# Gates kept in PSUM, a list schedule with new costs that picks engines, and a residual folded into a weight, in a four-layer graph network

## The chip, the cores and the metric

The kernel runs on one core of a Trainium2 chip. The metric is device time in microseconds (us). Its engines are TensorE (PE in the views; PEld is its weight load), VectorE (DVE), ScalarE (ACT), GpSimd (POOL) and SyncE (SP), which here only issues DMA. "Span" is the time from the first to the last instruction in the profiled execution; "median" is over the timed runs.

## The reference, cut to what matters

The input is 64 graphs of 256 nodes by 128 features, fp32, with one adjacency matrix. Four layers follow each other, each inside a residual and a layer norm:

```python
x = _layernorm(x + _L0_gnn_ref(x, adj, adj, ...))   # gated cell, five steps
x = _layernorm(x + _L1_gnn_ref(x, adj, ...))        # graph convolution, softmax adjacency
x = _layernorm(x + _L2_gnn_ref(x, adj, ...))        # attention, then an MLP
x = _layernorm(x + _L3_gnn_ref(x, adj, adj, ...))   # Chebyshev terms up to order 3
# one step of layer 0:
u3 = h @ u3_w.T + u3_b
z  = sigmoid(av @ w3_w.T + w3_b + u3)
r  = sigmoid(av @ w4_w.T + w4_b + u3)
hv = tanh(av @ w5_w.T + w5_b + (r * h @ u5_w.T + u5_b))
h  = (1.0 - z) * h + z * hv
```

In this case's data, the layer-2 parameters gat_g are all one and gat_b all zero.

## The kernel before

The kernel works on 32 pairs of graphs. It does not write its instructions in the order of the program: it adds each operation to a graph with an engine, a cost in ns, and the buffers it reads, writes and takes. Then a list scheduler in the kernel's own Python plays the program through with those costs and fixes the order of every engine's queue:

```python
LATENCY = {PE: 230, ACT: 80, DVE: 80, POOL: 120, SP: 1800}
...
    def order(self):
        ...
                for op in waiting[e]:
                    at = max(op.ready, clock[e])          # when it could start, in the model
                    ...
                    key = (at, op.rank)                   # earliest first, then the longest tail
            ...
            clock[op.eng] = at + op.cost
            end = at + op.cost + op.lat
```

On the chip each engine takes its queue strictly in that order, and semaphores hold an instruction back until its inputs are there. So a wrong cost gives no wrong result, only a queue whose head may wait while ready work stands behind it. A step of layer 0, cut:

```python
            tv, hv = bank(), flat("hv")                    # a PSUM bank; an SBUF tile
            add(PE, 865, ... matmul(tv.ap, w5s.ap, mT.ap ...), [mT, w5s], [tv], [tv, hv])
            add(PE, 865, ... matmul(tv.ap, u5h.ap, tr.ap ...), [tr, u5h], [tv])
            add(ACT, 690, ... activation(hv.ap, tv.ap, AF.Tanh, bias=bh.ap), [tv, bh], [hv])
            add(DVE, 735, ... tensor_sub(hv.ap, hv.ap, hT.ap), [hT], [hv])
            add(DVE, 735, ... scalar_tensor_tensor(hv.ap, tz.ap, 1.0, hv.ap, ...), [tz], [hv])
            add(DVE, 735, ... scalar_tensor_tensor(hT.ap, hv.ap, 0.5, hT.ap, ...), [hv], [hT])
            h = turn(add, hT, wide("htok"))                # VectorE transpose, then four DMAs
```

The new state of a step goes through `turn`: VectorE transposes in blocks, and SyncE issues four DMAs that put the blocks in place.

## Time and profile before

| | before |
|---|---|
| median | 1550.74 us of three runs (1551.2 of four beside the result, 1552.8 to 1553.2 beside the experiments) |
| PE / DVE / ACT / POOL busy | 98% / 71% / 63% / 31% |
| matmul records at the pace of their width | 1510.3 us |
| first matmul starts at | 5.9 us |
| gaps between records: to 150, 150 to 1250, 1250 to 1450, after 1450 us | 4.5, 1.3, 4.5, 18.3 us |
| from the last matmul's slot to the end | 6.3 us |

The last four rows add up to the span. A gap is what lies between the starts of two successive matmul records beyond the pace of the first one's width: 0.8333 ns a column plus 3.2 ns, which is within about 2 ns of the measured 429, 215 and 112 ns. All gaps below are worked out so from the start times in the traces.

### The profile page before, as it was taken

The page shows a single profiled execution, that of the slowest core. Times are in us where ns is not written, and L with a number is a line of the kernel's source. Part 1 is how long each engine was busy: PE and PEld are TensorE (multiplying, and loading weights), DVE is VectorE, ACT ScalarE, POOL GpSimd, SP SyncE. Part 2 cuts the span into 40 slices and gives each one's busy share as a digit, 9 for nine tenths or more (in the row PEclk, how much of TensorE's full clock was granted, in tenths as well). Part 3 has the DMA queues.
Part 4 walks back from the last instruction along what each step waited for, and adds up shares of the span by engine and source line. Part 5 has one row for each costly group of instructions (what it writes and reads, how often), then busy time and mean ns, then how long its engine had stood idle before and what let it go on. Part 6 is the DMA issues. An engine that isn't in the chain of part 4 may idle for free.

```text
span 1551.2 us, 21563 instructions
## 1 busy us (share of the span) xinstructions
PE 1522.9 (98%) x6364; PEld 1060.9 (68%) x6364; DVE 1106.7 (71%) x2579; ACT 972.0 (63%) x2198; POOL 487.1 (31%) x532
## 2 busy tenths in 40 slices
PE   8999999999999999999999999999999999999797
PEld 5556666667776676676676766676766776766686
DVE  4688776777666776666877666867667776877775
ACT  3344666666666676665766666666666666766663
POOL 0001232343323343223433223433223333423464
PEclk9999999999999999999999999999999999999999
DMA  7224445454355545445553556454445445545210
GB/s 246 43 35 64 72 75 79 80 93 80 65 89 101 90 72 92 74 87 93 91 88 58 91 88 102 75 93 76 78 89 89 77 77 86 95 74 83 42 22 28
DMA packets 725368, 125.33 MB, mean 81 GB/s; under 512 B 707844, under 2 KB 708612, under 8 KB 725124
## 3 DMA queue, kind: packets, MB, share of 16 engines
q1 hardware_dynamic: 724964, 123.42, 46.4%
q8 instruction: 52, 0.85, 0.2%
q14 instruction: 64, 0.52, 0.1%
q10 hardware_dynamic: 288, 0.53, 0.1%
HBM read 27.86 MB, written 8.45 MB: 23 GB/s over the span
## 4 chain that ended last, share of the span: by engine, by line
PE 94%; DVE 2%; POOL 1%; DMA 1%; SPq 1%; issue 0%; ACT 0%; POOLq 0%; DVEq 0%
PE ps L535 18%; PE ps L632 10%; PE ps L567 9%; PE ps L549 9%; PE ps L557 9%; PE ps L565 9%; PE ps L552 9%; PE ps L645 7%; PE ps L868 7%; PE ps L819 3%; PE ps L880 3%; PE ps L743 2%; SPq L515 1%; DMA sd<-line 1%; DVE u L780 0%; POOL rs L697 0%
## 5 line engine op out<-in xcount | busy, mean ns | idle before, releaser
L697 POOL TENSOR_TENSOR rs<-ss,neg_half 128x4 f32<-128x4 f32 (+1 forms) x140 | 155.5, 1111 | 518.6 <-DVE ss L690 509.9
L571 DVE TENSOR_TENSOR hv<-hv,hT 128x512 f32<-128x512 f32 x160 | 111.3, 696 | 184.9 <-ACT hv L569 184.0
L535 PE MATMUL ps<-aTs,htok 128*128 128x256 f32 x1024 | 242.3, 380 | 0.7 <-DMA htok<-S 0.5
L535 PEld LDWEIGHTS ps<-aTs,htok 128*128 128x128 f32 x1024 | 194.2, 190 | 62.5 <-issue 31.8
L538 ACT COPY mix<-ps 128x512 f32<-128x512 f32 x160 | 92.4, 583 | 156.6 <-PE ps L535 155.0
L567 PE MATMUL ps<-tr,u5h 128*128 128x512 f32 x320 | 163.4, 593 | 3.1 <-DVE tr L562 3.0
L552 PE MATMUL ps<-mix,w4s 128*128 128x512 f32 x320 | 163.1, 593 | 0.4 <-ACT mix L538 0.4
L557 PE MATMUL ps<-mix,dw 128*128 128x512 f32 x320 | 163.3, 593 | 0.0
L555 ACT ACTIVATE tr<-ps,br 128x512 f32<-128x512 f32 x160 | 109.0, 681 | 81.4 <-PE ps L552 76.3
L565 PE MATMUL ps<-mix,w5s 128*128 128x512 f32 x320 | 159.9, 593 | 0.0
L549 PE MATMUL ps<-hT,W 128*128 128x512 f32 x320 | 159.4, 593 | 0.0
L562 DVE SCALAR_TENSOR_TENSOR tr<-tr,hT 128x512 f32<-128x512 f32 x160 | 111.6, 698 | 44.2 <-ACT tr L555 43.5
L572 DVE SCALAR_TENSOR_TENSOR hv<-tz,hv 128x512 f32<-128x512 f32 x160 | 115.7, 723 | 35.2 <-ACT tz L560 33.7
L569 ACT ACTIVATE hv<-ps,bh 128x512 f32<-128x512 f32 x160 | 109.5, 684 | 48.9 <-PE ps L567 48.8
L560 ACT ACTIVATE tz<-ps,bz 128x512 f32<-128x512 f32 x160 | 109.9, 688 | 30.5 <-PE ps L557 30.1
L574 DVE SCALAR_TENSOR_TENSOR hT<-hv,hT 128x512 f32<-128x512 f32 x160 | 116.4, 728 | 2.2
L635 ACT COPY mix<-ps 128x512 f32<-128x512 f32 (+1 forms) x105 | 57.5, 549 | 89.0 <-PE ps L632 89.0
L509 DVE STREAM_TRANSPOSE S<-hT 128x512 f32<-128x512 f32 x160 | 109.9, 696 | 0.6
L552 PEld LDWEIGHTS ps<-mix,w4s 128*128 128x128 f32 x320 | 60.3, 190 | 54.3 <-issue 45.1
L688 DVE TENSOR_REDUCE ss<-sq 128x4 f32<-128x512 f32 (+1 forms) x140 | 85.9, 622 | 11.7 <-ACT sq L685 11.2
L645 PEld LDWEIGHTS ps<-W,mix 128*128 128x128 f32 x512 | 74.6, 192 | 28.2 <-issue 25.3
L663 POOL TENSOR_SCALAR rs<-mv 128x4 f32<-128x4 f32 (+1 forms) x70 | 31.1, 444 | 189.4 <-DVE mv L659 187.0
(213 smaller groups left out, 2964.3 us busy)
## 6 DMA issues: line engine op xcount, KB each, us to landing
htok<-S SPq DMA_DIRECT2D x640, 64.0 KB
xT<-S SPq DMA_DIRECT2D x232, 64.0 KB
wT<-S SPq DMA_DIRECT2D x116, 128.0 KB
xs<-xs_in SPq DMA_DIRECT2D x32, 256.0 KB
hT<-xT_in SPq DMA_DIRECT2D x32, 256.0 KB
dT<-S SPq DMA_DIRECT2D x116, 64.0 KB
sd<-line SPq DMA_DIRECT2D x29, 256.0 KB
zT<-S SPq DMA_DIRECT2D x116, 64.0 KB
```

What stands on the lines that cost most here:

```text
L535: nc.tensor.matmul(t.ap[:, b * N:(b + 1) * N], src.ap[:, 2 * b + j, :], m.ap[:, j, :], start=(j == 0), stop=(j == 1))
L549: add(PE, 865, lambda tg=tg: nc.tensor.matmul(tg.ap, mat("u3"), hT.ap, start=True, stop=False, skip_group_check=True), [hT, W0], [tg], [tg ...
L552: add(PE, 865, lambda tg=tg, mT=mT: nc.tensor.matmul(tg.ap, w4s.ap, mT.ap, start=False, stop=False, skip_group_check=True), [mT, w4s], [tg])
L557: add(PE, 865, lambda tg=tg, mT=mT: nc.tensor.matmul(tg.ap, dw.ap, mT.ap, start=False, stop=True, skip_group_check=True), [mT, dw], [tg])
L562: add(DVE, 735, lambda tr=tr: nc.vector.scalar_tensor_tensor(tr.ap, tr.ap, 1.0, hT.ap, op0=ALU.add, op1=ALU.mult), [hT], [tr])
L565: add(PE, 865, lambda tv=tv, mT=mT: nc.tensor.matmul(tv.ap, w5s.ap, mT.ap, start=True, stop=False), [mT, w5s], [tv], [tv, hv])
L567: add(PE, 865, lambda tv=tv, tr=tr: nc.tensor.matmul(tv.ap, u5h.ap, tr.ap, start=False, stop=True), [tr, u5h], [tv])
L572: add(DVE, 735, lambda hv=hv, tz=tz: nc.vector.scalar_tensor_tensor(hv.ap, tz.ap, 1.0, hv.ap, op0=ALU.add, op1=ALU.mult), [tz], [hv])
L574: add(DVE, 735, lambda hv=hv: nc.vector.scalar_tensor_tensor(hT.ap, hv.ap, 0.5, hT.ap, op0=ALU.mult, op1=ALU.add), [hv], [hT])
L632: nc.tensor.matmul(t.ap[:, b * N:(b + 1) * N], src.ap[:, 2 * b + j, :], m.ap[:, j, :], start=(j == 0), stop=(j == 1))
L645: nc.tensor.matmul(t.ap[:, c * D:(c + 1) * D], s(c), w, start=(k == 0), stop=(k == len(terms) - 1))
L697: nc.gpsimd.tensor_tensor(rs.ap, ss.ap, neg_half.ap[:, :C], op=ALU.pow)
```

## The change

Its intent was to give the scheduler better numbers and more freedom. Costs now follow the distance between starts of back-to-back instructions; a shared port of VectorE and GpSimd is modelled; some operations may run on either of two or three engines; the candidate gate stays in PSUM; layer 3's residual becomes an identity inside a weight; and the last pairs are handled differently.

```diff
-N_TAIL = 3
+N_TAIL = 2
-LATENCY = {PE: 230, ACT: 80, DVE: 80, POOL: 120, SP: 1800}
+EXTRA = [0, 0, 600, 0, 0]
+LATENCY = {PE: 205, ACT: 140, DVE: 130, POOL: 85, SP: 1800}
 def place(p):
-    return 20000 * min(p, 27) + 6000 * max(p - 27, 0)
+    return 20000 * min(p, 23) + 6000 * max(p - 23, 0)
     # in order(): the port, and operations that may go to several engines
+                    if entry[4]:
+                        at = max(at, shared - entry[4][0])
...
+            if port:
+                shared = at + sum(port)
     # layer 3: the residual within the weight
-        nc.vector.tensor_copy(vx.ap[:, 0, :], mat("v0"))
+        nc.vector.tensor_add(vx.ap[:, 0, :], mat("v0"), unswap.ap)
     # costs (some of many)
-            return 150 + 1.055 * n      # VectorE
-            return 250 + 0.745 * n + 93 * aps   # ScalarE
+        return 75 + 1.042 * n
+        return 100 + 0.8 * n + 93 * aps
-        add(DVE, 510 * C + 360, f, [sd, h2, mask], [u, mx, nm])
+        add(DVE, 415 * C + 280, f, [sd, h2, mask], [u, mx, nm], port=not by_pe)
-        add(ACT, 691 * C, f, [nm], [u, rd])
+        add(ACT, 491 * C, f, [nm], [u, rd])
     # layer 0: the candidate gate in PSUM
-            add(ACT, 690, ... activation(hv.ap, tv.ap, AF.Tanh, bias=bh.ap), [tv, bh], [hv])
-            add(DVE, 735, ... tensor_sub(hv.ap, hv.ap, hT.ap), [hT], [hv])
+            add(ACT, 545, ... activation(tv.ap, tv.ap, AF.Tanh, bias=bh.ap), [bh], [tv])
+            add(DVE, 609, ... tensor_sub(tv.ap, tv.ap, hT.ap), [hT], [tv])
     # engine choice, an example
-        add(POOL, 200 + 2.3 * C * D, lambda: nc.gpsimd.tensor_add(y.ap, x_t.ap, row("l1_bias", C)), ...)
+        two(add, C * D, lambda e: e.tensor_add(y.ap, x_t.ap, row("l1_bias", C)), ...)   # VectorE or GpSimd
```

## The prediction

> **What bounds the kernel now.** I read the page's busy times first, then who TensorE (PE) waited for, then the stretches, then the chain of the last 50 us.
>
> ```profile
> PE 1522.9 (98%) x6364; PEld 1060.9 (68%) x6364; DVE 1106.7 (71%) x2579; ACT 972.0 (63%) x2198; POOL 487.1 (31%) x532
> ```
>
> PE at 98% need not mean full speed, because matmuls are pipelined and their ends are modelled. So I took the start times of all 6364 matmul records. A record of 512 columns is followed by the next after 0.429 us (median), one of 256 columns after 0.215, one of 128 or 130 after 0.112. An fp32 product is two such records, so 512 columns cost 0.86 us, which the chain shows too:
>
> ```profile
> 1322.72 0.86 PE ps L567 x2
> 1323.58 0.86 PE ps L565 x2
> 1324.44 3.45 PE ps L868 x16
> ```
>
> Taking every record at the pace of its width, the sum is 1510.3 us (1600 of 512 columns, 2816 of 256, 1931 of 128 or 130). The rest of the 1551.2 us: the first matmul starts at 5.9 us, behind the load of the adjacency; 28.7 us are gaps between records beyond their pace; and from the last matmul's slot to the end of the span it takes 6.3 us (evacuation, norm, store). 1510.3 + 5.9 + 28.7 + 6.3 = 1551.2, which closes.
>
> In 50 us bins the gaps are: 4.5 us in the first 150 us (few pairs started); 1.3 us in all from 150 to 1250; 4.5 us from 1250 to 1400; 18.3 us after 1450. The stretches show the same:
>
> ```profile
> 400.00:600.00 200.00, 200.00 (x836) 139.86 (x835) 137.65 (x314) 128.59 (x289) 62.80 (x60) 1.00 0.49 84
> 1250.00:1300.00 50.00, 49.46 (x235) 37.39 (x234) 32.60 (x72) 32.22 (x75) 19.27 (x19) 1.00 0.55 90
> 1300.00:1350.00 50.00, 48.05 (x213) 34.19 (x213) 43.65 (x114) 38.33 (x95) 20.89 (x25) 1.00 0.48 80
> 1450.00:1480.00 30.00, 21.89 (x135) 19.10 (x135) 25.64 (x89) 19.29 (x57) 16.93 (x26) 0.89 0.20 35
> 1510.00:1520.00 10.00, 6.63 (x29) 5.29 (x29) 7.86 (x27) 3.90 (x11) 9.42 (x18) 0.84 0.01 2
> ```
>
> Columns after the length: busy us of PE, weight load, VectorE, ScalarE, GpSimd (records), granted clock, DMA share, GB/s. From 400 to 600 us PE is never idle, while VectorE is at 69% and ScalarE at 64%. It is idle at the end, where VectorE is the busy one (85% of 1450 to 1480), and from 1510 to 1520 GpSimd (94%). PE's own waits name the same places:
>
> ```profile
> PE ps L632 <- DVE x_t L669: 6.6, 2, 5.4
> PE ps L535 <- DMA aTs<-adjs_in: 5.9, 1, 5.9
> PE ps L567 <- DVE tr L562: 3.0, 2, 1.9
> PE ps L632 <- ACT hg L828: 2.9, 1, 2.9
> ```
>
> The largest is one wait of 5.4 us for a normalized tile that stood in VectorE's queue; the fourth is for a relu whose input came from GpSimd. So the kernel is bound by PE's arithmetic, plus a tail in which the last pairs' chains are too few and VectorE and GpSimd too busy.
>
> **What the Trainium skill says.** "Perfetto Trace Analysis", section Identifying the Most-Contended Engine, calls matmul busy time a poor measure and LDWEIGHTS busy a good one. Here they are 98% and 68%, and the start-to-start times side with the 98%: the 68% is no headroom. "TensorE: Matmul & The Clock Gate", section "Wait — 56ns, not 53.3ns?", gives a warm start-to-start of N / 2.4 GHz plus about 2.5 ns; an fp32 record here steps 429 ns at 512 columns, which fits if a record is two passes (2 x 213.3 + 2.5 = 429.2). The granted clock is 1.00, so only fewer matmuls or fewer gaps can help. "SBUF — State Buffer", section Who interferes with whom, says that a VectorE instruction with two SBUF inputs contends with a GpSimd instruction that reads SBUF, and that with at most one SBUF input (outside the two-port modes) it does not. The trace agrees in direction:
>
> ```profile
> L826 POOL TENSOR_TENSOR hg<-hg,rbc 128x512 f32<-128x512 f32 x29 | 46.9, 1618 | 2.3
> L727 POOL TENSOR_TENSOR y<-x_t,rbc 128x512 f32<-128x512 f32 x29 | 37.6, 1297 | 124.9 <-ACT x_t L678 101.0 <-DMA xT<-S 17.8 <-DMA htok<-S 6.1
> L574 DVE SCALAR_TENSOR_TENSOR hT<-hv,hT 128x512 f32<-128x512 f32 x160 | 116.4, 728 | 2.2
> L730 DVE TENSOR_TENSOR y<-ps,y 128x512 f32<-128x512 f32 x29 | 19.3, 667 | 9.6 <-PE ps L645 9.6
> ```
>
> The same GpSimd shape takes 1297 to 1618 ns, and VectorE's 128x512 takes 728 ns with both inputs in SBUF against 667 with one in PSUM. "ScalarE: Activation LUTs", section "Step-by-step: what each stage is for", says that ScalarE writes to PSUM with less latency than to SBUF. The kernel before has no such write, so no run shows it yet.
>
> **The change, part by part.**
>
> *PE work.* No matmul of a normal pair goes or comes. The residual of layer 3 becomes an identity added to a weight, in set-up; the product has the same shape. Only N_TAIL from 3 to 2 counts: a tail pair transposes on PE, per half-pair 4 x 2 tiles, 2 score columns and 4 attention tiles, so 14 one-record transposes, 28 a pair, at 0.112 us = 3.1 us; its four smaller products of layer 3 add under 0.1 us. PE's sum becomes 1510.3 - 3.2 = 1507.1.
>
> *Gates in PSUM.* Per step the tanh of the candidate is written in place and three VectorE operations take it from there. At 0.03 to 0.06 us saved on each (728 or 696 against 667), 160 steps x 3 x 0.045 = 22 us of VectorE's 1107, all beside PE: worth nothing where PE is gap-free. The price is the PSUM bank. Averaged over 160 steps, the tanh ends at 695.3 us and the last VectorE operation on it at 700.5, so a bank is held 5.2 us longer per step: 160 x 5.2 / 1551 = 0.54 of 8 banks on average. The step's banks hold now 3.4 (mix), 12.9 (gates) and 6.4 us (candidate), 22.7 us in all, 2.3 banks on average; layers 1 to 3 use some more. I expect no new wait from it.
>
> *Residual and evacuations.* The 58 additions of 415 ns (24 us, VectorE) become copies that ScalarE or VectorE may make; copies of mixes (51 + 92 us, ScalarE) may go to VectorE. Again beside PE, except in the tail.
>
> *Engine choice.* Adds and scalings can go to GpSimd, VectorE or ScalarE, whichever ends first in the model, with 600 ns against VectorE. That takes from VectorE in the tail, where PE waited for it, and from GpSimd the scale-and-shift pairs that it does alone now (1541 + 1618 ns a pair in a row).
>
> *Costs in the model.* The largest part, I think. The order of every queue is static and comes from these costs. The old ones overstate: 735 ns for a gate operation, where the timeline shows VectorE stepping by about 600 when it is not held; 691 ns for an exponential of 256 columns, now 491, where the timeline steps by 0.49 us. A schedule made with too slow VectorE and ScalarE is harmless where PE has a backlog and wrong where the chains are short, which is the tail. The last nine pairs instead of the last five are brought close in priority, so that more chains are open at the end.
>
> The sum: 1507.1 + 5.9 + 6.3 = 1519.3 us with no gap at all. Then the gaps: start 4.5 to 4 (cold clock and first loads stay); middle 1.3 to 1.5; 1250 to 1400 from 4.5 to 1.7; the tail from 18.3 to 6.5. That is 13.7 us, a choice of mine: the first two are set by loads and few open pairs, the last two by queues that the change aims at, so I halve them and a bit more. 1519.3 + 13.7 = 1533.0 us, 1.1% less.
>
> **Rivals.** (1) *PSUM becomes the bound.* If bursts fill the 8 banks, PE waits in the gap-free middle; 0.1 us a step would give back 16 us: 1549. Against it: 0.54 bank on average, and a scheduler that counts banks. (2) *Port contention.* More GpSimd operations beside VectorE's two-input ones lengthen both; GpSimd is the slower engine, about 1.3 us a tile against 0.7. If the tail's chains go through it, the tail keeps its 18 us and only the transposes are saved: 1551 - 3 - some 4 = 1544. For it: GpSimd was already 94% busy from 1510 to 1520. Against: the model now has the port. (3) *The tail is closed almost wholly*: gaps of 6 us, 1525. For it: at 85% VectorE has room as soon as some 5 us of its work goes elsewhere. (4) *Fewer tail pairs cost latency*: the third last pair now turns its tiles by DMA, and a score row's way through DMA takes over 4 us; if that pair ends last, 5 us come back: 1538.
>
> **Range and chances.** The floor of 1519.3 is all but 2% below 1550.7 (1519.7), so over 2% faster would need no gap or less arithmetic: 0.03. Slower by over 2% (above 1581.7) would need 62 us of new gaps, more than twice those of now: 0.02. Range 1523 to 1546.
>
> **What would show it right or wrong.** PE's records should sum to about 1507 us; the stretch 400 to 600 should still be 100% busy, or rival 1 holds; PE's idle time after 1450 should fall from 18 to below 10 us, or rival 2; VectorE should lose some 40 us and GpSimd gain. I am wrong if the middle gets gaps, or if the tail is as long as before.

## The result

The changed kernel takes 1592.8 us (median of four, 1589.8 to 1592.9) against 1551.2, so it is slower. The ratio is 1.0263, with a 95% interval of 1.0245 to 1.028. Ratios here are the mean time of one kernel's runs over that of the other's runs of the same rounds, so they are not quite the ratio of the medians quoted. The prediction, 1533 within 1523 to 1546 and at 95% "within 2%", was wrong.

The page's busy line and the start of its chain, after the change:

```profile
PE 1532.0 (96%) x6328; PEld 1047.1 (66%) x6328; DVE 1193.2 (75%) x2649; ACT 878.4 (55%) x1890; POOL 462.7 (29%) x538
...
PE 59%; DVE 21%; SPq 6%; DMA 5%; POOL 4%; issue 3%; ACT 2%; DVEq 0%; POOLq 0%; ACTq 0%
```

And the start of the chain before the change:

```profile
PE 94%; DVE 2%; POOL 1%; DMA 1%; SPq 1%; issue 0%; ACT 0%; POOLq 0%; DVEq 0%
```

Before, the chain that ended last was PE and hardly anything else. Now 36% of it runs through VectorE, the DMA queue, DMA and GpSimd. Busy time alone hides this: 96% still looks like a bound PE. VectorE gained 86 us of busy time, where I had expected it to lose 40; ScalarE lost 94, and GpSimd, which was to gain, lost 24.

The stretches after the change (length, then busy us and records of PE, PEld, DVE, ACT, POOL; clock; DMA share; GB/s):

```profile
400.00:600.00 200.00, 190.42 (x780) 129.58 (x780) 152.91 (x324) 107.34 (x226) 61.98 (x66) 1.00 0.48 80
1000.00:1200.00 200.00, 200.00 (x768) 131.61 (x767) 136.99 (x278) 109.79 (x224) 41.32 (x45) 1.00 0.45 74
...
1450.00:1500.00 50.00, 49.82 (x233) 37.64 (x232) 37.47 (x92) 29.70 (x64) 22.97 (x29) 1.00 0.48 73
1500.00:1550.00 50.00, 49.17 (x287) 43.26 (x286) 38.34 (x127) 35.11 (x99) 26.60 (x41) 1.00 0.29 55
```

From 400 to 600 us PE ran 780 records where it had run 836, at the same clock. The tail, on the other hand, is as tight as hoped. One stretch of the middle, 1000 to 1200, has no gap at all; there GpSimd did a third less than from 400 to 600. In terms of the sum:

| us | before | predicted | after |
|---|---|---|---|
| records at pace | 1510.3 | 1507.1 | 1507.2 |
| first matmul | 5.9 | 5.9 | 6.1 |
| gaps to 150 | 4.5 | 4 | 8.4 |
| gaps 150 to 1250 | 1.3 | 1.5 | 47.6 |
| gaps 1250 to 1450 (predicted: to 1400) | 4.5 | 1.7 | 8.1 |
| gaps after 1450 | 18.3 | 6.5 | 8.0 |
| end | 6.3 | 6.3 | 5.8 |

Who PE waited for, after the change (us, times, longest):

```profile
PE ps L613 <- DVE tr L608: 29.2, 25, 1.6
PE ps L920 <- ACT mix L561: 6.3, 11, 1.3
PE ps L581 <- DMA aTs<-adjs_in: 6.1, 1, 6.1
```

L613 is the product that needs r * h, which VectorE makes in L608. Its wait comes back about once in 49 us, at the pace of one pair. At 500.5, 548.8, 599 and so on the same product is up to 1.8 us late, each time behind the layer-3 products.

### Where one of these waits comes from

The kernel's scheduling routine gives each operation a planned start. I ran that routine and laid the plan beside the trace: the operations of each engine come in the same order in both, so every one can be matched. The before kernel's plan ends at 1549.2 us; PE stays within about 6 us of it all the way. The changed kernel's plan ends at 1530.2 us; PE is 10 us late at a planned 174 us, 26 at 481, 49 at 962, and 58 at 1520, so most of the loss falls in the first two thirds.

The wait at 500.5 us goes back to PE itself, 39 us before. Along that loop (times in us, "late" is actual minus planned):

```
                                            planned   actual    late
PE    L932 layer-3 product, ends             439.2    461.9     22.7
DVE   L608 gate of another pair, ends        446.3    469.2     22.9
DVE   L832 masked maximum, ends              449.4    473.1     23.8
DVE   L894 relu plus residual, ends          451.8    476.3     24.5
SP    L539 four DMA issues (wT), end         460.3    485.3     25.0
SP    L539 four DMA issues (xT), end         463.0    488.5     25.5
SP    L539 four DMA issues (htok), end       465.7    491.3     25.5
DVE   L764 addition on that htok, starts     467.5    493.6     26.1
DVE   L608 the gate waited for, ends         474.5    500.4     25.9
PE    L613                        starts     474.9    500.5     25.6
```

So one round adds 2.9 us, read along this chain. About 0.9 are VectorE's masked maximum, 0.7 another VectorE operation, and some 1.6 DMA issue and landing; a few tenths come back where latencies were overstated. As the loop closes through PE, nothing makes it up, and the next round adds its own.

The VectorE part, instruction by instruction (timeline of VectorE, then of GpSimd; start, us, engine, line):

```profile
469.11 1.49 DVE L832 CUSTOM_DVE_ANT_0 u<-sd,maskb 128x256 f32<-128x256 f32 x1
...
470.53 1.48 DVE L832 CUSTOM_DVE_ANT_0 u<-sd,maskb 128x256 f32<-128x256 f32 x1
...
471.94 0.41 DVE L832 CUSTOM_DVE_ANT_0 u<-sd,maskb 128x256 f32<-128x256 f32 x1
```

```profile
468.67 1.65 POOL L876 TENSOR_TENSOR hg<-hg,rbc 128x512 f32<-128x512 f32 x1 [0.80 <-DVE hg L749]
470.39 1.33 POOL L877 TENSOR_TENSOR hg<-hg,rbc 128x512 f32<-128x512 f32 x1
```

The same instruction takes 0.41 us alone and 1.49 while GpSimd is on a two-input operation; the first two end about when GpSimd's do. The model has a port, but as a lock held for a whole operation, and it lets the next operation on it start only when the one before is planned to end. Here GpSimd's first operation was planned at 1.24 us and took 1.65, so L832's first instruction still met it. L832 is one operation to the scheduler and ten instructions on the chip; GpSimd's second operation, planned behind all ten, got in between them. Over the whole run the groups were, before and after:

```profile
L780 DVE CUSTOM_DVE_ANT_0 u<-sd,maskb 128x256 f32<-128x256 f32 x116 | 47.3, 463 | 23.3 <-DMA sd<-line 23.2
L842 DVE SCALAR_TENSOR_TENSOR hb<-hb,y 128x512 f32<-128x512 f32 x29 | 20.4, 704 | 1.0
```

```profile
L832 DVE CUSTOM_DVE_ANT_0 u<-sd,maskb 128x256 f32<-128x256 f32 x120 | 81.0, 728 | 0.5 <-DMA sd<-line 0.2
L894 DVE SCALAR_TENSOR_TENSOR hb<-hb,y 128x512 f32<-128x512 f32 x30 | 34.7, 1155 | 0.1
```

As a group, the masked maximum of a full pair was planned at 2.40 us before and took 2.07 on average; after, it was planned at 1.94 and took 3.20.

The DMA part (SyncE's queue):

```profile
481.60 3.68 SPq L539 DMA_DIRECT2D wT<-S  x4
485.39 3.10 SPq L539 DMA_DIRECT2D xT<-S  x4
488.60 2.65 SPq L539 DMA_DIRECT2D htok<-S  x4
```

Four issues are planned at 2.73 us; these took 3.68, 3.10 and 2.65 (mean over the run 2.84, and 2.78 before). The landing is planned at 1.80; here the consumer started 2.4 us after the last issue ended (median of the consumers that sat waiting 1.9). The means are hardly different before, where PE was not held up: there one wait of 0.5 us on such a transfer is all that PE shows.

### The profile page after: what moved, and what is told of

The parts are those of the page before. It is cut to its first block, busy times and chain, and to the rows that moved or that the text cites. A ratio compares the mean times of both kernels' runs of the same rounds, so it can differ in the third digit from the quotient of the medians.

```text
span 1591.2 us, 21200 instructions
## 1 busy us (share of the span) xinstructions
PE 1532.0 (96%) x6328; PEld 1047.1 (66%) x6328; DVE 1193.2 (75%) x2649; ACT 878.4 (55%) x1890; POOL 462.7 (29%) x538
## 4 chain that ended last, share of the span: by engine, by line
PE 59%; DVE 21%; SPq 6%; DMA 5%; POOL 4%; issue 3%; ACT 2%; DVEq 0%; POOLq 0%; ACTq 0%
PE ps L581 13%; PE ps L613 6%; SPq L539 6%; PE ps L598 5%; PE ps L595 5%; PE ps L603 5%; PE ps L672 5%; PE ps L611 4%; PE ps L920 4%; DMA htok<-S 4%; PE ps L685 4%; DVE S L533 3%; PE ps L932 3%; PE ps L871 2%; DVE ps L618 2%
## 5 line engine op out<-in xcount | busy, mean ns | idle before, releaser
L561 ACT COPY mix<-ps 128x512 f32<-128x512 f32 (+1 forms) x253 | 145.1, 574 | 220.4 <-PE ps L581 141.5
L613 PE MATMUL ps<-tr,u5h 128*128 128x512 f32 x320 | 168.0, 607 | 29.2 <-DVE tr L608 29.2
L744 POOL TENSOR_SCALAR ss<-ss 128x4 f32<-128x4 f32 (+1 forms) x102 | 23.5, 231 | 482.5 <-DVE ss L736 482.4
L745 POOL TENSOR_TENSOR rs<-ss,neg_half 128x4 f32<-128x4 f32 (+1 forms) x136 | 135.6, 998 | 75.2 <-DVE ss L738 66.6
L608 DVE SCALAR_TENSOR_TENSOR tr<-tr,hT 128x512 f32<-128x512 f32 x160 | 119.9, 749 | 46.9 <-ACT tr L601 42.6
L616 ACT ACTIVATE ps<-ps,bh 128x512 f32<-128x512 f32 x160 | 104.1, 651 | 87.5 <-PE ps L613 87.4
L617 DVE TENSOR_TENSOR ps<-ps,hT 128x512 f32<-128x512 f32 x160 | 109.8, 686 | 43.3 <-ACT ps L616 41.3
L618 DVE SCALAR_TENSOR_TENSOR ps<-tz,ps 128x512 f32<-128x512 f32 x160 | 109.5, 686 | 20.8 <-ACT tz L606 19.1
L613 PEld LDWEIGHTS ps<-tr,u5h 128*128 128x128 f32 x320 | 56.7, 189 | 100.2 <-DVE tr L608 57.8
L620 DVE SCALAR_TENSOR_TENSOR hT<-ps,hT 128x512 f32<-128x512 f32 x160 | 108.6, 680 | 2.7
```

Of the source, the lines that this page charges most:

```text
L561: add(ACT, act(n) - 45, lambda: nc.scalar.copy(o(), i()), *args).also = [(DVE, dve(n), lambda: nc.vector.tensor_copy(o(), i()), None)]
L608: add(DVE, 609, lambda tr=tr: nc.vector.scalar_tensor_tensor(tr.ap, tr.ap, 1.0, hT.ap, op0=ALU.add, op1=ALU.mult), [hT], [tr], port=True)
L613: add(PE, 865, lambda tv=tv, tr=tr: nc.tensor.matmul(tv.ap, u5h.ap, tr.ap, start=False, stop=True), [tr, u5h], [tv])
L617: add(DVE, 609, lambda tv=tv: nc.vector.tensor_sub(tv.ap, tv.ap, hT.ap), [hT], [tv])
L618: add(DVE, 609, lambda tv=tv, tz=tz: nc.vector.scalar_tensor_tensor(tv.ap, tz.ap, 1.0, tv.ap, op0=ALU.add, op1=ALU.mult), [tz], [tv])
L745: nc.gpsimd.tensor_tensor(rs.ap, ss.ap, neg_half.ap[:, :C], op=ALU.pow)
```

## The experiments

The theory (T): the new costs are close to an undisturbed start-to-start time, so the plan has no margin. It fills queues so that any instruction longer than planned, by a collision or by a late DMA, reaches PE. Rivals: the candidate gate holds PSUM banks too long; the new engine mix is at fault, not the costs; DMA alone; or the changed order is just an unlucky draw. Each run had three rounds, with the kernel before timed on the same chip, and each gave a correct result.

### e1: the gate back in SBUF, same order

```diff
-            tv = bank()
+            tv, hv = bank(), flat("hv")
-            add(ACT, 545, ... activation(tv.ap, tv.ap, AF.Tanh, bias=bh.ap), [bh], [tv])
+            add(ACT, 545, ... activation(hv.ap, tv.ap, AF.Tanh, bias=bh.ap), [tv, bh], [hv])
     # and the three VectorE operations on hv, costs unchanged
```

> The changed kernel with the candidate gate back in SBUF: the scheduler's order on every engine is the very same list (I compared the two lists), only the storage of the tanh and of three VectorE operands differs. If the longer hold of PSUM banks is what stalls TensorE (rival 1 of the prediction), the time falls towards 1535. If the cause is the order made with tight costs, it stays at about 1593, or rises by up to 10 us because VectorE's three operations per step then have two SBUF inputs and meet GpSimd on the port.

Measured: 1613.3 us, ratio 1.0388 (1.0371 to 1.0406). The PSUM rival falls: in this order, the gate in PSUM is worth 20 us (1613.3 less 1592.8), twice as much as I had allowed for. Its gaps add up to 92.3 us. Two of the groups that changed, changed kernel and then this one:

```profile
L608 DVE SCALAR_TENSOR_TENSOR tr<-tr,hT 128x512 f32<-128x512 f32 x160 | 119.9, 749 | 46.9 <-ACT tr L601 42.6 <-DMA dT<-S 4.1
L618 DVE SCALAR_TENSOR_TENSOR ps<-tz,ps 128x512 f32<-128x512 f32 x160 | 109.5, 686 | 20.8 <-ACT tz L606 19.1
```

```profile
L608 DVE SCALAR_TENSOR_TENSOR tr<-tr,hT 128x512 f32<-128x512 f32 x160 | 127.4, 796 | 44.3 <-ACT tr L601 44.3
L618 DVE SCALAR_TENSOR_TENSOR hv<-tz,hv 128x512 f32<-128x512 f32 x160 | 113.5, 710 | 22.2 <-ACT tz L606 20.7
```

With both inputs in SBUF again L618 is only 24 ns longer on average, but its longest takes 1756 ns, where none took over 737 with one input in PSUM. L608, which the edit does not touch and which PE waits for, grows more: 19 of its 160 take over 900 ns in both runs, 15 or 16 of them beside one GpSimd operation (L749), and those take about 1195 ns in the changed kernel and 1566 here. That this is what cost the 20 us is read from the traces, not tested.

### e2: a margin of 15% on VectorE, ScalarE and GpSimd

```diff
-            op = g.add(eng, cost, fn, (p, n[0]), reads, writes, takes)
+            op = g.add(eng, cost if eng in (PE, SP) else cost * 1.15, fn, (p, n[0]), reads, writes, takes)
     # and the same factor on the costs of an operation's other engines
```

> The changed kernel, with only the scheduler's costs of VectorE, ScalarE and GpSimd operations times 1.15 (engine choice, port model, gates in PSUM, place and N_TAIL as changed). Theory T (the new costs leave no margin, so whatever takes longer than modelled reaches TensorE once a round): the gaps of 45.6 us from 150 to 1200 us fall below 5 us and the time is 1530 to 1545, below the kernel before. Contention theory (the new mix of GpSimd and VectorE work is the cause): more work goes to GpSimd, so it stays above 1575. PSUM theory: stays at about 1590.

Measured: 1557.5 us, ratio 1.0031 (1.0016 to 1.0046). The direction is T's and the contention theory's 1575 is missed, though GpSimd was given more to do. But I had expected 1530 to 1545: gaps of 16.8 us stayed from 150 to 1250. In the loops behind them, as I traced them back, the largest overrun is now DMA issue (19 us), which had been given no margin. So T needed an addition, that the margin must cover the DMA too; e8 tests it.

### e3: the same order, two GpSimd operations cut to one column

```diff
-        two(add, C * D, lambda e: e.tensor_mul(hg.ap, hg.ap, row("gat_g", C)), [rbc], [hg])
-        two(add, C * D, lambda e: e.tensor_add(hg.ap, hg.ap, row("gat_b", C)), [rbc], [hg])
+        two(add, C * D, lambda e: e.tensor_mul(hg.ap[:, :, :1], hg.ap[:, :, :1], row("gat_g", C)[:, :, :1]), [rbc], [hg])
+        two(add, C * D, lambda e: e.tensor_add(hg.ap[:, :, :1], hg.ap[:, :, :1], row("gat_b", C)[:, :, :1]), [rbc], [hg])
```

> The changed kernel in the same order, but the two GpSimd operations that scale and shift by gat_g and gat_b touch one column in 128 only (gat_g is one and gat_b zero, so the result stays right). That takes away the long two-input GpSimd reads beside VectorE's masked maximum (3.20 us a group of ten instructions against 1.94 modelled). If port contention starts the stall, that group falls to about 2.1 us and the time by some 15 to 25 us, to 1568 to 1578. If DMA alone does, it stays above 1588.

Measured: 1565.2 us, ratio 1.0078 (1.0063 to 1.0093); 28 us off, a little more than expected. The plan is the same list, so nothing but the durations can have done it. The masked maximum is back to 1.9 us a group, as planned:

```profile
L832 DVE CUSTOM_DVE_ANT_0 u<-sd,maskb 128x256 f32<-128x256 f32 x120 | 44.7, 427 | 0.3 <-DMA sd<-line 0.3
```

L894 is back at 726 ns as well. What stays, 22.0 us of gaps from 150 to 1250, is again behind DMA issue, as far as the trace tells. This is no fair kernel, since it leans on the data. It also makes the two operations themselves shorter (about 1440 ns to 360), which could have helped in its own right. A replay speaks against that. It is an estimate: it lets each operation of the plan's order start when its engine, its inputs and its buffers are free, with durations from the traces. With the changed kernel's own durations it ends at 1603 us (the chip: 1591), with e3's durations for GpSimd alone at 1604, and with e3's for VectorE alone at 1573. So, by this estimate, e3 measures the collision.

### e4: tight costs, engines as before

```diff
-        op = add(*a, *args)
-        op.also, op.port = [(*b, (60, pool(n) - 80))], (75, dve(n) - 75)
+        op = add(*(b if on == POOL else a), *args)
+        op.port = (60, pool(n) - 80) if on == POOL else (75, dve(n) - 75)
     # on=POOL for the four operations that were on GpSimd; no operation keeps an alternative
```

> The changed kernel with the tight costs, but no engine choice: every operation on the engine that it had before (additions of layer 3's residual still gone). Theory T: the middle still has gaps, time 1560 to 1600. If the engine choice alone is the fault: 1530 to 1540, the middle gap-free.

Measured: 1580.1 us, ratio 1.0175 (1.0156 to 1.0193). 27 us of loss stay without the engine choice, so the mix alone is not the cause. The 13 us between this run and the changed kernel are not the price of the choice, because the order is another one too: gaps from 150 to 1250 are down to 24.3 us, but those from 1250 to 1450 are up to 22.5.

### e5: the kernel before, with only the costs of the change

```diff
-LATENCY = {PE: 230, ACT: 80, DVE: 80, POOL: 120, SP: 1800}
+LATENCY = {PE: 205, ACT: 140, DVE: 130, POOL: 85, SP: 1800}
-            add(DVE, 735, ...)
+            add(DVE, 609, ...)
     # and so on for every cost that the change touched; nothing else
```

> The kernel before, with nothing changed but the scheduler's costs and latencies, which are those of the change (engines, gates in SBUF, N_TAIL 3, place 27 as before). Its own list schedule then expects 1539.5 us in place of 1549.2. Theory T (tight costs are enough to lose): slower than before, 1565 to 1600, with gaps from 150 to 1250 us of over 15 us where the kernel before has 1.3. If the tight costs are harmless and the new engine mix is at fault: 1540 to 1552.

Measured: 1583.5 us, ratio 1.0194 (1.0172 to 1.0216). Numbers that no instruction ever sees, only the scheduler, cost 30 us. Gaps from 150 to 1250 are 18.5 us where the kernel before has 1.3; they also grow at the start (9.3), from 1250 to 1450 (9.2) and in the tail (22.0). This is the clearest run that tight costs alone lose time. It does not single out one collision. The masked maximum is as short as before (448 ns against 463); here it is r * h (L562) that meets GpSimd: 23 of its 160 take over 900 ns, 22 of them beside the same GpSimd operation (L826). Before, and then e5:

```profile
L562 DVE SCALAR_TENSOR_TENSOR tr<-tr,hT 128x512 f32<-128x512 f32 x160 | 111.6, 698 | 44.2 <-ACT tr L555 43.5
```

```profile
L562 DVE SCALAR_TENSOR_TENSOR tr<-tr,hT 128x512 f32<-128x512 f32 x160 | 132.6, 829 | 92.0 <-ACT tr L555 92.0
```

The same replay as in e3 ends at 1582 us with this run's durations (the chip: 1581.5). As estimates from it: r * h kept to 690 ns wins back 1.5 us, DMA issue as planned 5, and all VectorE operations kept to their planned cost 23. So many overruns on VectorE share the loss, and which of them a tight order exposes differs from order to order.

### e6: the kernel before, with only the gate in PSUM

The edit is e1's the other way round, on the kernel before, with its costs of 690 and 735.

> The kernel before, with only the candidate gate kept in PSUM (costs as before; the scheduler's order comes out identical). Every theory left says that the middle has no gap to win, so 1549 to 1553; less in the tail at most. If PSUM gates cost banks it would be above 1556.

Measured: 1551.8 us, ratio 0.9988 (0.9973 to 1.0003), no difference. The order is the same list as before. Where PE has no gap, shorter VectorE work is worth nothing; in e1's order it was worth 20 us.

### e7: the DMA charged in full, costs still tight

```diff
-LATENCY = {PE: 205, ACT: 140, DVE: 130, POOL: 85, SP: 1800}
+LATENCY = {PE: 205, ACT: 140, DVE: 130, POOL: 85, SP: 2450}
-        add(SP, 2730, f, [S], [dst], [dst])
+        add(SP, 2900, f, [S], [dst], [dst])
```

> The changed kernel, with only the DMA of a turn modelled as the trace has it: 2.90 us for its four issues in place of 2.73, and 2.45 us to landing in place of 1.80. If the DMA's underestimate is the main cause, 1540 to 1560. If VectorE's collisions with GpSimd are the main one, as the run with the cut GpSimd work said (28 us of 42), it gains under 15 us: 1578 to 1595.

Measured: 1560.1 us, ratio 1.0045 (1.003 to 1.006). My expectation was wrong: it gained 33 us, not under 15. I had also called the numbers "as the trace has it", while they are near its slower cases (means 2.84 and 1.9). They are a margin on the DMA. But this run does not isolate the DMA, because the order is a new one. The masked maximum takes 462 ns here instead of 728, so most of its collisions went as well. Gaps from 150 to 1250 are 13.6 us.

### e8: both margins

The edits of e2 and e7 together.

> The changed kernel with both: costs of VectorE, ScalarE and GpSimd times 1.15 and the true DMA of a turn. In the run with the margin alone, the chains behind the 21 us of remaining gaps from 150 to 1450 us held 19 us of DMA issue time over the model. If that is right, they mostly close: 1535 to 1548, faster than the kernel before.

Measured: 1539.0 us, ratio 0.9907 (0.989 to 0.9923), faster than the kernel before by 0.9%, and 54 us faster than the changed kernel with only costs edited. The middle is full again:

```profile
400.00:600.00 200.00, 200.00 (x838) 139.84 (x837) 140.53 (x310) 118.78 (x249) 66.60 (x71) 1.00 0.50 85
```

VectorE has 70% and GpSimd 33% to do here, more on GpSimd than in the changed kernel (31%). So it is not the amount of GpSimd work that decides, but when it meets VectorE and how much room there is.

### e9: tight costs in another order

```diff
-N_TAIL = 2
+N_TAIL = 3
-    return 20000 * min(p, 23) + 6000 * max(p - 23, 0)
+    return 20000 * min(p, 27) + 6000 * max(p - 27, 0)
```

> The changed kernel with N_TAIL 3 and place 27 as before, all else as changed: again tight costs, but another order (its own schedule expects 1538.3 us). Theory T: the middle stalls as well, 20 to 60 us of gaps from 150 to 1200 us, 1575 to 1605 in all. If the changed order was only an unlucky draw, this one is near 1545.

Measured: 1607.5 us, ratio 1.0351 (1.0336 to 1.0367), just above the expected range. Gaps from 150 to 1250 are 54.3 us. So the changed order was not a single unlucky draw: another tight one loses as much in the middle, and e4 and e5 are two more that lose.

### e10: the kernel before, with only the tail's numbers

The edit of e9 the other way round, on the kernel before.

> The kernel before with only N_TAIL 2 and place 23 of the change, loose costs kept (its own schedule expects 1545.2 us against 1549.2). The transposes' 3.2 us go and the middle stays gap-free: 1544 to 1549. If the DMA latency of the third last pair ate it, 1550 or more.

Measured: 1549.3 us, ratio 0.9976 (0.9959 to 0.9993). The transposes' 3.2 us are won, and no more. The gaps after 1450 fall from 18.3 to 3.2 us, but those from 1250 to 1450 rise from 4.5 to 18.5, with waits for the turned state on top (here with the loose costs; 8.5 of the 9.2 us fall from 1250 to 1450):

```profile
PE ps L535 <- DMA htok<-S: 9.2, 6, 4.0
```

So with old costs, the new placing only moved the tail's wait to an earlier place, some 150 us before.

### e11 and e12: a larger margin, and one aimed at the collision

e11 is e8 with 1.20 in place of 1.15. e12 is e8 with one more edit:

```diff
-        add(DVE, 415 * C + 280, f, [sd, h2, mask], [u, mx, nm], port=not by_pe)
+        add(DVE, 415 * C + 1280, f, [sd, h2, mask], [u, mx, nm], port=not by_pe)
```

> As the run with margin 1.15 and the true DMA (1539.0), margin 1.20. Its own schedule expects 1537.6 in place of 1532.7. If the margin is already enough at 1.15, more of it only dulls the tail: 1538 to 1548.

> As the run with margin 1.15 and the true DMA, and the masked maximum charged 1 us more, about what it lost to GpSimd in the changed kernel (3.20 against 1.94 us). Of the 20 us of gaps left, 3.5 are from 150 to 1450 chains and some 6 lie before 150: at most 3 us are to be won: 1535 to 1543.

Measured: e11 1548.8 us, ratio 0.9973 (0.9958 to 0.9988); e12 1536.5 us, ratio 0.9895 (0.988 to 0.9909), the lowest median of all; e11 is just above its expected range. More margin everywhere lost 10 us, and not in the tail as I had written, but in the middle (9.6 us of gaps from 150 to 1250). There r * h collides again: from 330 to 946 us PE waits 0.4 to 1.8 us for it once a pair, 14 times, each time after an L608 of about 1.38 us beside a GpSimd operation. e8, and then e11:

```profile
L608 DVE SCALAR_TENSOR_TENSOR tr<-tr,hT 128x512 f32<-128x512 f32 x160 | 117.4, 734 | 63.3 <-ACT tr L601 58.7
```

```profile
L608 DVE SCALAR_TENSOR_TENSOR tr<-tr,hT 128x512 f32<-128x512 f32 x160 | 124.7, 780 | 49.7 <-ACT tr L601 49.4
```

So a margin does not see to it that the collisions fall where they do no harm, and the amount of it has to be tried. e12's median is 2.5 us below e8's, but that is not shown as a gain: the intervals of the two ratios overlap, the runs were on different chips, and the order is a new one. e12's last stretches:

```profile
1450.00:1500.00 50.00, 50.00 (x301) 45.53 (x300) 36.42 (x119) 33.51 (x95) 31.39 (x46) 1.00 0.26 54
1500.00:1534.00 34.00, 25.07 (x143) 21.57 (x141) 16.87 (x54) 13.43 (x36) 15.64 (x30) 0.95 0.07 24
```

Its sum is 1507.2 + 5.8 + 15.6 of gaps + 5.8 = 1534.3 us, the profiled span.

### All of them beside their own plan

| run | plan ends | median | plan missed by | gaps 150 to 1250 |
|---|---|---|---|---|
| before | 1549.2 | 1551 to 1553 | 2 to 4 | 1.3 |
| after | 1530.2 | 1592.8 | 63 | 47.6 |
| e1 gate in SBUF | 1530.2 | 1613.3 | 83 | 61.6 |
| e2 margin 1.15 | 1533.0 | 1557.5 | 25 | 16.8 |
| e3 GpSimd cut | 1530.2 | 1565.2 | 35 | 22.0 |
| e4 old engines | 1531.7 | 1580.1 | 48 | 24.3 |
| e5 before, tight | 1539.5 | 1583.5 | 44 | 18.5 |
| e6 before, gate in PSUM | 1549.2 | 1551.8 | 3 | 0.0 |
| e7 DMA charged | 1530.3 | 1560.1 | 30 | 13.6 |
| e8 margin and DMA | 1532.7 | 1539.0 | 6 | 1.6 |
| e9 tight, tail 3 | 1538.3 | 1607.5 | 69 | 54.3 |
| e10 before, tail 2 | 1545.2 | 1549.3 | 4 | 2.6 |
| e11 margin 1.20 and DMA | 1537.6 | 1548.8 | 11 | 9.6 |
| e12 margin, DMA, collision | 1535.8 | 1536.5 | 1 | 1.8 |

"Plan ends" is what each kernel's own scheduling routine returns. The plans with loose costs, or with margin and DMA both, come true within 11 us; those with tight costs miss by 35 to 83, and those with only one of the two margins (e2, e7) by 25 and 30.

What could not be tried is the DMA's overrun taken away in the changed order alone. A version that issued half of a turn's DMAs leaves part of a tile unwritten. So how the 42 us split between collisions and DMA in that order stays open: e3 shows that without the collisions of two operations 28 go, and the rest has DMA issue in its loops, but that last part is read from the trace, not tested. The replay of e3, as an estimate, gives 31 us for L832 and L894 at their planned cost, 20 for DMA issue as planned, and 37 for both together, so the two overlap.

## Why the prediction was wrong

**What held.** The account of PE was right to a tenth: 1507.2 us of records at pace for the predicted 1507.1, 6.1 before the first matmul, 5.8 at the end. The floor of 1519.3 was not broken. The tail closed much as I had chosen, 8.0 us of gaps after 1450 for the predicted 6.5, but not by the costs that I called the largest part: costs alone left it at 22.0 (e5), and the placing with fewer tail pairs alone brought it to 3.2, with 18.5 moved to before 1450 (e10). In that the size was luck. PSUM banks were no bound, as argued against rival 1, though its signature, a middle below 100%, appeared for another reason; e1 tells the two apart.

**The step that failed** is "Costs in the model". I wrote that the old costs "overstate" and that "a schedule made with too slow VectorE and ScalarE is harmless where PE has a backlog and wrong where the chains are short". I treated the backlog as a property of the kernel. The runs showed that it is made by the overstatement: e5 changes nothing but the costs and loses 30 us. The overstatement was the margin that took up collisions and late DMAs, both of which were there before (the masked maximum's plan of 2.40 us against 2.07, DMA issue of 2.78 against a planned 2.73). So the gap terms "middle 1.3 to 1.5" and "1250 to 1400 from 4.5 to 1.7" were wrong by 46 and about 6 us, and "start 4.5 to 4" by 4. The chance of a loss was also misread: "62 us of new gaps" is the sum of all gaps above the floor of 1519.3, of which the kernel before already had 28.7, so 34 new ones were enough. The run has 72.1 in all.

**Rival 2 was in the wrong place.** I looked for the port contention in the tail and counted "the model now has the port" against it. The model's port is held for an operation, the chip's for an instruction, so a group of ten lets GpSimd in. It bit in the middle, where e3 puts it at 28 us.

**Gates in PSUM.** I priced them at 22 us of VectorE time, "worth nothing where PE is gap-free". The durations fell by 10, 37 and 48 ns (696, 723, 728 to 686, 686, 680), 15 us in 160 steps where I had 22. The second half is right for the kernel before (e6) and missed the changed one, which is not gap-free: 20 us (e1).

**Engine choice.** I wrote that VectorE would lose some 40 us. Its busy time rose by 86, and GpSimd's fell by 24 where it was to gain. Of the 86, 34 are the masked maximum and 14 the relu with residual, both waiting at the port; work taken from ScalarE is in the rest (one form of normalization, new on VectorE, is 24 us).

**Tail pairs.** The 3.2 us of transposes came as worked out (e10). Rival 4, a third last pair that waits for DMA, is not separated from the placing; e10 shows waits for turned states of 9.2 us.

**Signs named beforehand.** "The stretch 400 to 600 should still be 100% busy" and "I am wrong if the middle gets gaps" were the right things to watch: it was 95%.

## What to carry to other kernels

A static order on in-order queues is only as good as its slack. In this kernel, costs near the undisturbed times made a plan that looked shorter and lost, because an overrun on a loop through the busiest engine is paid, and little of it is won back. Give costs a margin where durations scatter (shared ports, DMA), lay the plan beside the trace and look at where lateness grows, and stop when the plan comes true; here 15% with the DMA charged in full turned a loss of 2.6% into a gain of 0.9% (e8; 1.05% in e12), while 20% gave most of that away. And before calling costs "overstated", ask what the overstatement is paying for.

## What the Trainium skill lacked or had wrong

- "SBUF — State Buffer", section Who interferes with whom: right that two-input VectorE instructions contend with GpSimd's reads and those with one SBUF input do not: L618 took at most 737 ns with one input in PSUM and up to 1756 with two in SBUF (e1). It gives no time for these forms. A 128x256 two-input VectorE instruction took 0.41 us alone and 1.49 beside a two-input GpSimd operation, and ended 0.3 us after it.
- "Perfetto Trace Analysis", section Identifying the Most-Contended Engine: of the two measures of headroom that it names, LDWEIGHTS busy time misled for this fp32 kernel. It is 68% in the kernel before, where PE's records run at their pace for 97% of the span (1510.3 of 1551.2 us). The start-to-start time of the records was the measure that worked. The other measure, MFU, was not worked out here.
- "TensorE: Matmul & The Clock Gate": the section read, on the 56 ns start-to-start, gives no fp32 pace, though the skill counts the passes of fp32 elsewhere. The trace has an fp32 product as two records, each with a start-to-start of 429 ns at 512 columns, 215 at 256 and 112 at 128.
- "ScalarE: Activation LUTs", section "Step-by-step: what each stage is for": right that writing to PSUM is faster. In the same order, the tanh of 128x512 from PSUM took 684 ns into SBUF (before) and 659 into PSUM (e6); in the changed order 680 (e1) and 651 (after).
- None of the pages read says that the costs of a static schedule need a margin; e5 puts its absence at 30 us of 1553.
